# Plane copies, PSUM banks and convolution weights moved within the first pass of a two-layer attention kernel

## The chip, the cores and the metric

The kernel runs on one core of a Trainium2 chip. A core has a matrix engine (TensorE, PE in the profile), a vector engine (VectorE, DVE), a scalar engine (ScalarE, ACT), a general engine (GpSimd, POOL) and a queue that mostly issues transfers (SyncE, SP). Each works through its own instructions in their order and waits for the others by semaphores. The metric is the device time of one execution in microseconds (us), as the median of several runs.

## The reference

x has 8 images of 256 channels and 64 x 64 pixels. Two layers are applied, each added to its input.

```python
# layer 0: attention over a coarse grid
xr = conv(x, w_sr, stride 4)             # 16 x 16 positions
xr = (xr - mean) / sqrt(var + eps) * norm_g + norm_b
q = w_q @ x ; k, v = split(w_kv @ xr)    # 8 heads of 32
out = softmax(q k^T * 32**-0.5) v
x = x + gamma_s * (w_out @ out)
# layer 1: linear attention
qkv = w_qkv @ x                          # 768 channels
agg = w_pw (grouped 8 x 8) of depthwise 5 x 5 of qkv
q, k, v = groups of 8 of [qkv, agg] ; q, k = relu
kv = k^T [v, 1] ; att = q kv / (its last column + eps)
x = x + batchnorm(w_proj @ att)
```

All of it is in float32.

## The kernel before

Three passes follow each other. The first computes layer 0 and layer 1's qkv and writes q, k and v to DRAM as "planes" (q and k on a padded grid), `kd` and `vd`; the second does the depthwise and grouped convolutions and the sums k^T v; the third divides and projects. Only the first is touched.

The first pass (`first_pass`) walks over 128 steps n = (image b, strip s of 512 pixels, half c of the channels, which is four heads): 16 iterations per image. In the loop at the end of the function one iteration writes down, in this order: the first scores (`scores(..., 0, ...)`, L832: 16 matrix products into four PSUM banks, then four exponentials, L844); the work kept in `late`; for step n-1 the products with v (`valued`, L863) and the counting of the softmax sums (`counted`, L888); the second scores (`scores(..., 1, ...)`) with four more exponentials; copies of the products with v (`copied`, L895, on ScalarE) and their division (`normed`: transposes L904 on VectorE, reciprocal, product L910); then up to seven products of layer 1's qkv (L972), two or four taps of the convolution of the next image (`keys_values`, L738), the next q (L815), and for every second step the output projection (`added`, L925, L926).

Layer 1's qkv of a pair of strips (g) is three groups of seven products (pair 1, pair 2, pair 0), written down over four iterations as 7, 4, 7 and 3. A group combines products on VectorE (`part`, L1041, L1045, L1054), beginning with a copy of the first product by ScalarE (L1034). Pair 1 (k) writes a tile `whole` (L988), which one iteration later is transposed (`turn`, L992) and copied by ScalarE into the padded plane (`inside`, L998: the plane copies, four per group). Planes, k and v are then stored (`stored`, L1005, L1015, L1020). `new_stages` (L951, L952) clears the borders on GpSimd.

PSUM has eight banks. `bank` takes the first of a list and puts it at the end at once; a bank that is kept (the two of the products with v, the one of the convolution) comes back to the end of the list only with `given_back`. So the place of that call decides which earlier tile a later product must wait for.

The convolution of the next image runs over iterations 6 to 9 of an image, two taps at two places in each, with one weight tile of 256 KB per tap in three buffers (`wsr`, L735). Images 1 to 7 are done so; that of image 0 stands alone at the start.

The order on each queue is not only that of the program. A scheduler may move an instruction within its engine's stream where no data forbid it; `tc.keep_in_program_order` pins an instruction behind the one that was written down just before it on the same engine, and does not pin that other one.

```python
    def given_back(keep):
        turns.append(kept.pop(keep))
```

Of the kernel before, what the change touches and what calls it, by code (L numbers as in the profile page):

```python
# [32 lines left out]
P = 128  # L33
# [3 lines left out]
R = 4  # L37
# [582 lines left out]
def phase(dy, dx):  # L620

    return dy // 2 * 8 + dx // 2 * 4 + dy % 2 * 2 + dx % 2
# [4 lines left out]
def first_pass(ctx: ExitStack, tc: tile.TileContext, a, fine, planes, x2d, kd, vd, ready):  # L627
# [94 lines left out]
            tc.keep_in_program_order(nc.sync.dma_start(v[1 : NB2 + 1, i], src[:NB2]))  # L722


    kks, vvs = {}, {}

    def keys_values(b):
        ln = lambda name: keys.tile([P, 2, NK], F32, tag="ln", name=f"{name}_{b}", bufs=2)
        xr = ln("xr")

        ps = bank(f"sr_{b}", "sr").rearrange("p (o k) -> p o k", o=2)
        taps = sorted((phase(dy, dx), dy * R + dx) for dy in range(R) for dx in range(R))
        for f, tap in taps:
            w = keys.tile([P, 2, C], F32, tag="wsr", name=f"wsr_{b}_{f}", bufs=3)
            nc.sync.dma_start(w, a.w_sr[:, :, tap])  # L735
            for ci in range(2):
                for oc in range(2):
                    nc.tensor.matmul(  # L738
                        ps[:, oc],
                        w[:, ci, oc * P : (oc + 1) * P],  # L740
                        strips(b, f // 2)[:, ci, f % 2 * NK : (f % 2 + 1) * NK],
                        start=(f == ci == oc == 0),
                        stop=(f == R * R - 1 and ci == 1),
                        skip_group_check=True,
                    )
            yield
        nc.scalar.copy(xr, ps)
        given_back("sr")
        yield

        mean = bank(f"mean_{b}")[:, :NK]
        for ci in range(2):
            nc.tensor.matmul(mean, mean_w, xr[:, ci], start=(ci == 0), stop=(ci == 1))
        for ci in range(2):
            nc.vector.tensor_sub(xr[:, ci], xr[:, ci], mean)
        sq = ln("sq")
        nc.vector.tensor_mul(sq, xr, xr)
        yield

        var = bank(f"var_{b}")  # L760
        for kc in range(2):
            for ci in range(2):
                nc.tensor.matmul(
                    var[:, kc : kc + 1],
                    sq[:, ci, kc * P : (kc + 1) * P],
                    mean_w[:, 0:1],
                    start=(ci == 0),
                    stop=(ci == 1),
                )
        rstd = two.tile([P, 2, 2], F32, tag="rstd", name=f"rstd_{b}")  # L770
        nc.vector.tensor_scalar_add(rstd[:, 0], var[:, 0:2], LN_EPS)
        nc.gpsimd.tensor_tensor(rstd[:, 1], rstd[:, 0], mhalf, ALU.pow)
        wide = keys.tile([P, 2, P], F32, tag="wide", name=f"wide_{b}", bufs=1)
        nc.scalar.copy(wide, rstd[:, 1].unsqueeze(2).to_broadcast([P, 2, P]))
        yield
        yield
        rs = bank(f"rs_{b}")[:, :NK]
        for kc in range(2):
            nc.tensor.matmul(rs[:, kc * P : (kc + 1) * P], wide[:, kc], ident, start=True, stop=True)
        for ci in range(2):  # L780
            nc.vector.tensor_mul(xr[:, ci], xr[:, ci], rs)
            nc.vector.tensor_scalar(
                xr[:, ci], xr[:, ci], consts["vec"][:, 0, ci : ci + 1], consts["vec"][:, 1, ci : ci + 1], ALU.mult, ALU.add
            )
        yield
        kk = two.tile([P, 2, NK], F32, tag="kk", name=f"kk_{b}")
        vv = two.tile([P, 4, C], F32, tag="vv", name=f"vv_{b}")
        kks[b], vvs[b] = kk, vv
        for oc in range(2):
            ps = bank(f"k_{b}_{oc}")[:, :NK]  # L790
            for ci in range(2):
                nc.tensor.matmul(
                    ps, consts["wkv"][:, ci, oc * P : (oc + 1) * P], xr[:, ci], start=(ci == 0), stop=(ci == 1)
                )
            nc.scalar.copy(kk[:, oc], ps)
        yield
        for kc in range(2):
            ps = bank(f"v_{b}_{kc}")[:, :C]
            for ci in range(2):
                nc.tensor.matmul(  # L800
                    ps, xr[:, ci, kc * P : (kc + 1) * P], consts["wkv"][:, ci, C:], start=(ci == 0), stop=(ci == 1)
                )
            for h, rows in enumerate(HALVES):
                nc.scalar.copy(vv[rows, 2 * kc + h], ps[rows])
        for h, rows in enumerate(HALVES):
            nc.sync.dma_start(vv[HALVES[1 - h], h::2], vv[rows, h::2])
        yield
# [18 lines left out]
    def scores(b, s, c, kc, qs):  # L826
        scs = [bank(f"sc_{b}_{s}_{c}_{kc}_{h}") for h in range(4)]
        for kq in range(2 * kc, 2 * kc + 2):
            for h in range(4):
                rows = slice(h * D0, (h + 1) * D0)  # L830
                for half in range(2):
                    nc.tensor.matmul(  # L832
                        scs[h][HALVES[half], QH[kq % 2]],
                        kks[b][rows, c, kq * P // 2 : (kq + 1) * P // 2],
                        qs[rows, QH[half]],
                        start=True,
                        stop=True,
                    )
        es = []
        for h in range(4):  # L840
            if h % 2 == 0:
                e = two.tile([P, 2, 2, QB // 2], F32, tag="e", name=f"e_{b}_{s}_{c}_{kc}_{h}", bufs=E_BUFS)
                es.append(e)
            nc.scalar.activation(e[:, h % 2].rearrange("p q n -> p (q n)"), scs[h], AF.Exp, scale=D0**-0.5)  # L844
        return es

    sums, att = {}, {}

    late = []

    def catch_up():
        was, late[:] = list(late), []
        for f in was:
            f()
# [30 lines left out]
    def counted(b, s, c, es):  # L885
        for h in range(4):
            for half, rows in enumerate(HALVES):
                nc.tensor.matmul(  # L888
                    sums["av"][half][h * D0 : (h + 1) * D0, QH[1]], ones_w[rows], es[h // 2][rows, h % 2], start=True, stop=True
                )  # L890

    def copied(b, s, c):
# [64 lines left out]
    def qkv(b, g, pair):  # L957
# [21 lines left out]
        def ended(r, h, u, ps, op=ALU.add):  # L979
            if stages:  # L980
                y, x = g // 2, g % 2
                inside = stages[r][:, 2 * h : 2 * h + 2, y : y + NB, x : x + NB]
            rows = lambda t: t.rearrange("p (f y x) -> p f y x", f=2, y=NB)
            if not turned:
                nc.vector.tensor_tensor(inside, rows(u), rows(ps), op)  # L985
                return
            whole = halves.tile([P, QB], F32, tag="whole", name=f"whole_{name}_{r}_{h}", bufs=6)
            nc.vector.tensor_tensor(whole, u, ps, op)  # L988

            def turn():  # L990
                tc.keep_in_program_order(
                    nc.vector.transpose(  # L992
                        turned[r][:, :, 2 * h : 2 * h + 2].rearrange("p y f e -> p f y e"),
                        whole.rearrange("p (f y e) -> p f y e", f=2, y=NB // 2),
                    )
                )
                if stages:
                    tc.keep_in_program_order(nc.scalar.copy(inside, rows(whole)))  # L998

            late.append(turn)  # L1000

        def stored(r):
            j = js[r]
            if stages:
                nc.sync.dma_start(  # L1005
                    planes[b, j].rearrange("g (k i f) e -> g k i (f e)", k=4, i=D1)[:, g],
                    stages[r].rearrange("p f y x -> p (f y x)"),
                )
            if not turned:
                return  # L1010
            for k in range(4):
                n, src = 4 * (j % 2) + k, turned[r][k * D0 : (k + 1) * D0].rearrange("p y f e -> p y (f e)")
                if j < 4:
# [7 lines left out]

        def ready(r):
            if turned:
                late.append(lambda: stored(r))
            else:
                stored(r)

# [70 lines left out]
    for n in range(n_all + 6):  # L1098
# [2 lines left out]
        filled = now and n // 16 + 1 < B  # L1101
        if filled and at == 5 and n > 16:
            load_x(n // 16 + 1)
        if filled and at == 6:
            ahead = keys_values(n // 16 + 1)
        if now and at == (10 if n < 16 else 1):
            border(n // 16)

# [2 lines left out]
            ej[n] = joined(*order[n], e0)  # L1111
        if (n, 0) in blank:
            new_stages(*blank.pop((n, 0)), 0)
        catch_up()
        if was:
            p = order[n - 1]
            for kc in range(2):
                valued(*p, kc, es[n - 1][kc])
            counted(*p, ej.pop(n - 1))
            es.pop(n - 1)  # L1120
        if now:
            es[n] = e0, scores(*order[n], 1, q.pop(n))
            joined_too(ej[n], es[n][1])
        if (n, 1) in blank:
            new_stages(*blank.pop((n, 1)), 1)
        if was:
            copied(*p)
            normed(*p)

        products = todo.pop(n, [])  # L1130
        taps = 2 if filled and 6 <= at < 10 else 0
# [922 lines left out]
```

## Time and profile before

| | |
|---|---|
| median of three runs | 3593.32 us (3591.59 to 3598.89) |
| profiled execution, its own time | 3592.86 us |
| its span, first to last instruction | 3591.0 us |
| TensorE busy | 3490.9 us, 97% |
| VectorE, GpSimd, ScalarE busy | 2261.4, 1865.7, 1478.1 us |
| mean granted TensorE clock | 0.989 |

The first pass ends near 1960 us of the span. A row of the timeline has the start, the length, the engine, the line, the operation, the tiles it writes and reads, their shapes and how many equal instructions were merged; in brackets, the idle time before it and what ended that. A row of the waits has the engine and line that waited, what it waited for, the total, how often, and the longest. "PEq", "SPq" and so on are an engine's sequencer, "PEld" the loading of weights into TensorE. In float32 each matrix product appears as two instructions.

### The profile page before, as it was taken

The numbers are of one execution on the slowest core, as the hardware profiler recorded it, in microseconds if no ns is written. First come the engines' busy times: TensorE is split into PE (matmuls) and PEld (weight loads), VectorE is DVE, ScalarE is ACT, GpSimd is POOL, SyncE is SP. The second block draws the span as 40 slices with busy tenths as digits, with TensorE's granted clock in tenths as the row PEclk, the third lists the DMA queues.
The fourth block names the chain that finished last, engine by engine and source line by source line (L and its number), as shares of the span: only waits on it lengthen the run. The fifth ranks groups of instructions, "written<-read, shape, count | busy, mean of one in ns | idle before, by whom it ended". The sixth has DMA issues, their size and how long they took to land.

```text
span 3591.0 us, 91344 instructions
## 1 busy us (share of the span) xinstructions
PE 3490.9 (97%) x38050; PEld 2109.8 (59%) x38050; DVE 2261.4 (63%) x3499; ACT 1478.1 (41%) x3385; POOL 1865.7 (52%) x1762
## 2 busy tenths in 40 slices
PE   8999999999999999999998999999999999999998
PEld 5554555545545555455444788888888873333333
DVE  1567476575674765765777777777777774544442
ACT  2345354353443443544553444444444423333322
POOL 3557466465564664655764566656656541222222
PEclk9999999999999999999999999999999999999999
DMA  5345445455454453553655999989999987787773
GB/s 181 99 117 150 132 106 161 107 157 135 106 155 124 109 163 105 156 133 94 162 123 142 269 265 263 266 253 253 264 263 260 260 245 210 223 236 225 231 216 93
DMA packets 577192, 647.27 MB, mean 180 GB/s; under 512 B 81665, under 2 KB 452865, under 8 KB 576769
## 3 DMA queue, kind: packets, MB, share of 16 engines
q1 hardware_dynamic: 576768, 641.34, 64.5%
q8 instruction: 301, 4.93, 0.6%
q14 instruction: 123, 1.00, 0.1%
HBM read 389.85 MB, written 249.23 MB: 178 GB/s over the span
## 4 chain that ended last, share of the span: by engine, by line
PE 86%; DMA 6%; DVE 2%; ACT 2%; issue 1%; SPq 1%; POOL 1%; POOLq 0%; DVEq 0%; ACTq 0%
PE qkv L972 15%; PE p L1772 11%; PE cv L1345 8%; PE sc L832 7%; PE cv L1376 6%; PE av L863 6%; PE sums L1431 6%; PE sr L738 6%; PE o L925 6%; PE q L815 6%; PE rep L1758 2%; PE av L888 2%; DMA vq<-v 1%; DMA wsr<-in_w_sr_dram 1%; PE den L1739 1%
## 5 line engine op out<-in xcount | busy, mean ns | idle before, releaser
L883 POOL TENSOR_TENSOR ef<-ef,e 128x512 f32<-128x512 f32 x512 | 687.5, 1353 | 149.4 <-ACT e L844 126.2
L844 ACT ACTIVATE e<-sc 128x512 f32<-128x512 f32 x1024 | 529.7, 608 | 509.4 <-PE sc L832 509.3
L876 POOL TENSOR_TENSOR ef<-e 128x512 f32<-128x512 f32 x256 | 333.1, 1320 | 516.2 <-ACT e L844 476.2
L1782 POOL TENSOR_TENSOR y<-z,xs 128x512 f32<-128x512 f32 x128 | 165.4, 1301 | 459.3 <-ACT z L1780 438.7
L1345 PE MATMUL cv<-w,c 128*128 128x128 f32 x3072 | 387.1, 279 | 8.6 <-DVE stage L985 6.1
L1345 PEld LDWEIGHTS cv<-w,c 128*128 128x128 f32 x3072 | 364.5, 194 | 10.4 <-issue 6.1
L904 DVE STREAM_TRANSPOSE rden<-av 128x256 f32<-128x256 f32 x256 | 99.6, 428 | 339.8 <-ACT att L895 339.8
L972 PE MATMUL qkv<-differences,combined 128*128 128x512 f32 x576 | 291.2, 597 | 11.0 <-ACT e L844 10.4
L832 PE MATMUL sc<-q,kk 32*64 32x256 f32 x8192 | 288.3, 388 | 0.0
L1431 PE MATMUL sums<-vq,r 128*32 128x288 f32 x4096 | 265.6, 408 | 0.1
L738 PE MATMUL sr<-x,wsr 128*128 128x256 f32 x1024 | 239.0, 388 | 20.0 <-DMA wsr<-in_w_sr_dram 19.9
L1772 PE MATMUL p<-raw,wp 128*128 128x512 f32 x512 | 248.8, 608 | 6.5 <-ACT z L1780 6.4
L863 PE MATMUL av<-e,vv 64*32 64x256 f32 x8192 | 252.0, 379 | 0.7 <-ACT e L844 0.5
L1362 ACT ACTIVATE r<-s 128x512 f32<-128x512 f32 x128 | 80.9, 632 | 416.6 <-DVE s L1361 415.0
L832 PEld LDWEIGHTS sc<-q,kk 32*64 32x64 f32 x8192 | 152.1, 131 | 153.3 <-issue 105.0
L815 PE MATMUL q<-x,wq 128*128 128x512 f32 x512 | 242.0, 594 | 0.0
L738 PEld LDWEIGHTS sr<-x,wsr 128*128 128x128 f32 x1024 | 197.8, 194 | 75.0 <-issue 24.9
L1772 PE MATMUL p<-agg,wp 128*128 128x512 f32 x512 | 241.0, 593 | 0.0
L925 PE MATMUL o<-att,wout 128*128 128x512 f32 x512 | 230.4, 592 | 0.0
L823 ACT COPY q<-q 128x512 f32<-128x512 f32 x128 | 75.1, 587 | 352.2 <-PE q L815 352.2
L1376 PE MATMUL cv<-y,w 128*128 128x128 f32 x1536 | 204.4, 279 | 3.6 <-DVE y L1297 3.2
L910 DVE TENSOR_TENSOR att<-att,rall 128x512 f32<-128x512 f32 x128 | 204.9, 1600 | 4.4
(163 smaller groups left out, 6070.6 us busy)
## 6 DMA issues: line engine op xcount, KB each, us to landing
planes<-stage SPq DMA_DIRECT2D x128, 578.0 KB
d<-planes SPq DMA_DIRECT2D x128, 578.0 KB
vq<-v SPq DMA_DIRECT2D x256, 256.0 KB
raw<-planes SPq DMA_DIRECT2D x64, 578.0 KB
x<-in_xp_dram SPq DMA_DIRECT2D x64, 512.0 KB
wsr<-in_w_sr_dram SPq DMA_DIRECT2D x128, 256.0 KB
x<-x SPq DMA_DIRECT2D x128, 256.0 KB
k<-turned SPq DMA_DIRECT2D x256, 128.0 KB
```

The costliest lines, as they stand in the source:

```text
L738: nc.tensor.matmul(ps[:, oc], w[:, ci, oc * P : (oc + 1) * P], strips(b, f // 2)[:, ci, f % 2 * NK : (f % 2 + 1) * NK], start=(f == ci == ...
L815: nc.tensor.matmul(ps, consts["wq"][:, ci, c * P : (c + 1) * P], strips(b, s)[:, ci], start=(ci == 0), stop=(ci == 1),)
L832: nc.tensor.matmul(scs[h][HALVES[half], QH[kq % 2]], kks[b][rows, c, kq * P // 2 : (kq + 1) * P // 2], qs[rows, QH[half]], start=True, sto ...
L844: nc.scalar.activation(e[:, h % 2].rearrange("p q n -> p (q n)"), scs[h], AF.Exp, scale=D0**-0.5)
L863: nc.tensor.matmul(sums["av"][half][cols, : QB // 2], vvs[b][rows, kq, c * P + h * D0 : c * P + (h + 1) * D0], es[h // 2][rows, h % 2, kq ...
L883: tc.keep_in_program_order(nc.gpsimd.tensor_tensor(f, f, e[:, :, half], ALU.add))
L925: nc.tensor.matmul(ps, consts["wout"][:, c, oc * P : (oc + 1) * P], att[c], start=(c == 0), stop=(c == 1))
L972: nc.tensor.matmul(ps, w, x, start=True, stop=True)
L1345: nc.tensor.matmul(ps[:, g * P : (g + 1) * P], c[:, g, cols], w[:, g, n * P : (n + 1) * P], start=(da == 0), stop=(da == 1),)
L1376: nc.tensor.matmul(out, w[:, g], x, start=True, stop=True)
L1431: nc.tensor.matmul(ps[h * D0 : (h + 1) * D0, : 36 * D1].rearrange("p (r n e) -> p r n e", r=3, e=D1), kt[:, par, h, 2 * r + c], vq[:, r : ...
L1772: nc.tensor.matmul(as_block(ps, i // 2), wp[:, i, oc * P : (oc + 1) * P], block(g, i // 2, i % 2, j), start=(i == 0), stop=(i == 3),)
```

## The change

Four things are edited in the first pass.

- The plane copies of pair 1 and the stores of those planes go into a second list, `later`, which is worked off after the second scores and their exponentials; `late` stays where it was.
- `copied` and `normed` of step n-1 are written down ahead of the second scores, so the two banks of the products with v are given back before the second scores take theirs.
- The convolution's weights: three taps are loaded at iteration 5 (with a first `next(ahead)` there), and each tap's products are followed by the load of the tap three further on. The loads are pinned in SP's queue.
- The products of scores, of counting and of the convolution are pinned in program order. The products with v are not.

```diff
+        for f in range(3):
+            load_tap(f)
+        if b:
+            yield
         ps = bank(f"sr_{b}", "sr").rearrange("p (o k) -> p o k", o=2)
-        taps = sorted((phase(dy, dx), dy * R + dx) for dy in range(R) for dx in range(R))
-        for f, tap in taps:
-            w = keys.tile([P, 2, C], F32, tag="wsr", name=f"wsr_{b}_{f}", bufs=3)
-            nc.sync.dma_start(w, a.w_sr[:, :, tap])
+        for f in range(R * R):
+            w = ws.pop(f)
             for ci in range(2):
                 for oc in range(2):
-                    nc.tensor.matmul(
...
+                    pinned(
+                        nc.tensor.matmul(
...
+            load_tap(f + 3)
             yield
```

```diff
+        def load_tap(f):
+            if f < R * R:
+                ws[f] = keys.tile([P, 2, C], F32, tag="wsr", name=f"wsr_{b}_{f}", bufs=3)
+                tc.keep_in_program_order(nc.sync.dma_start(ws[f], a.w_sr[:, :, taps[f][1]]))
```

`scores` and `counted` put `pinned(...)` around their `nc.tensor.matmul` in the same way. In `qkv` and in the loop:

```diff
-                if stages:
-                    tc.keep_in_program_order(nc.scalar.copy(inside, rows(whole)))
+
+            def inner():
+                tc.keep_in_program_order(nc.scalar.copy(inside, rows(whole)))
 
             late.append(turn)
+            if stages:
+                later.append(inner)
...
             if turned:
-                late.append(lambda: stored(r))
+                late.append(lambda: turned_stored(r))
+                if stages:
+                    later.append(lambda: stored(r))
             else:
                 stored(r)
...
-        if filled and at == 6:
+        if filled and at == 5:
             ahead = keys_values(n // 16 + 1)
+            next(ahead)
...
-        catch_up()
+        catch_up(late)
         if was:
             p = order[n - 1]
             for kc in range(2):
                 valued(*p, kc, es[n - 1][kc])
             counted(*p, ej.pop(n - 1))
             es.pop(n - 1)
+            copied(*p)
+            normed(*p)
         if now:
             es[n] = e0, scores(*order[n], 1, q.pop(n))
             joined_too(ej[n], es[n][1])
+        catch_up(later)
         if (n, 1) in blank:
             new_stages(*blank.pop((n, 1)), 1)
-        if was:
-            copied(*p)
-            normed(*p)
```

`stored` now only stores planes; `turned_stored` holds the stores of k and v.

More of the change, by code (lines that the diff above doesn't have):

```diff
@@ L722, in border @@
             tc.keep_in_program_order(nc.sync.dma_start(v[1 : NB2 + 1, i], src[:NB2]))
+    pinned = tc.keep_in_program_order
     kks, vvs = {}, {}
@@ L729, in keys_values @@
         xr = ln("xr")
+        taps = sorted((phase(dy, dx), dy * R + dx) for dy in range(R) for dx in range(R))
+        ws = {}
+        def load_tap(f):
[6 more added lines that the diff above has]
+            yield
         ps = bank(f"sr_{b}", "sr").rearrange("p (o k) -> p o k", o=2)
-        taps = sorted((phase(dy, dx), dy * R + dx) for dy in range(R) for dx in range(R))
-        for f, tap in taps:
-            w = keys.tile([P, 2, C], F32, tag="wsr", name=f"wsr_{b}_{f}", bufs=3)
-            nc.sync.dma_start(w, a.w_sr[:, :, tap])
+        for f in range(R * R):
+            w = ws.pop(f)
             for ci in range(2):
                 for oc in range(2):
[L738 to L744, printed above, removed]
+                    pinned(
+                        nc.tensor.matmul(
+                            ps[:, oc],
+                            w[:, ci, oc * P : (oc + 1) * P],
+                            strips(b, f // 2)[:, ci, f % 2 * NK : (f % 2 + 1) * NK],
+                            start=(f == ci == oc == 0),
+                            stop=(f == R * R - 1 and ci == 1),
+                            skip_group_check=True,
+                        )
                     )
+            load_tap(f + 3)
             yield
@@ L831, in scores @@
                 for half in range(2):
[L832 to L837, printed above, removed]
+                    pinned(
+                        nc.tensor.matmul(
+                            scs[h][HALVES[half], QH[kq % 2]],
+                            kks[b][rows, c, kq * P // 2 : (kq + 1) * P // 2],
+                            qs[rows, QH[half]],
+                            start=True,
+                            stop=True,
+                        )
                     )
@@ L847, in first_pass, with catch_up @@
     sums, att = {}, {}
-    late = []
-    def catch_up():
+    late, later = [], []
+    def catch_up(late):
         was, late[:] = list(late), []
@@ L887, in counted @@
             for half, rows in enumerate(HALVES):
-                nc.tensor.matmul(
-                    sums["av"][half][h * D0 : (h + 1) * D0, QH[1]], ones_w[rows], es[h // 2][rows, h % 2], start=True, stop=True
+                pinned(
+                    nc.tensor.matmul(
+                        sums["av"][half][h * D0 : (h + 1) * D0, QH[1]],
+                        ones_w[rows],
+                        es[h // 2][rows, h % 2],
+                        start=True,
+                        stop=True,
+                    )
                 )
@@ L996, in turn, with turned_stored @@
                 )
-                if stages:
-                    tc.keep_in_program_order(nc.scalar.copy(inside, rows(whole)))
+            def inner():
+                tc.keep_in_program_order(nc.scalar.copy(inside, rows(whole)))
             late.append(turn)
+            if stages:
+                later.append(inner)
         def stored(r):
-            j = js[r]
[L1004 to L1010, printed above, removed]
+            nc.sync.dma_start(
+                planes[b, js[r]].rearrange("g (k i f) e -> g k i (f e)", k=4, i=D1)[:, g],
+                stages[r].rearrange("p f y x -> p (f y x)"),
+            )
+        def turned_stored(r):
+            j = js[r]
             for k in range(4):
```

## The prediction

> **What bounds the kernel now.** I read the page first, then the waits of TensorE in the first pass, then the timeline around those waits. The page says that TensorE (PE) is the busy engine:
>
> ```profile
> PE 3490.9 (97%) x38050; PEld 2109.8 (59%) x38050; DVE 2261.4 (63%) x3499; ACT 1478.1 (41%) x3385; POOL 1865.7 (52%) x1762
> ```
>
> No other engine is near, so only time in which PE stands can be won. The table of stretches puts 1832.04 of 1865.00 us busy between 70 and 1935 us, the first pass without its start and end. What PE waits for there:
>
> ```profile
> PE qkv L972 <- ACT e L844: 19.4, 31, 1.3
> PE sr L738 <- DMA wsr<-in_w_sr_dram: 11.8, 7, 2.2
> ```
>
> 31 waits of products for an exponential, and 7 for convolution weights: the two places that the change touches. Busy ends are modelled, so I take losses from distances between starts. An undisturbed iteration beside one with plane copies (PE timeline):
>
> ```profile
> 964.61 1.98 PE L972 MATMUL qkv<-x,wqkv 128*128 128x512 f32 x4
> 966.43 1.02 PE L972 MATMUL qkv<-differences,combined 128*128 128x512 f32 x2
> 967.29 1.89 PE L800 MATMUL v<-wkv,xr 128*128 128x256 f32 x8
> ...
> 978.67 1.98 PE L972 MATMUL qkv<-x,wqkv 128*128 128x512 f32 x4
> 981.09 1.13 PE L972 MATMUL qkv<-differences,combined 128*128 128x512 f32 x2 [0.43 <-ACT e L844]
> 982.05 1.88 PE L815 MATMUL q<-x,wq 128*128 128x512 f32 x4
> ```
>
> Three products take 967.29 - 964.61 = 2.68 us undisturbed, and 982.05 - 978.67 = 3.38 in the other: 0.70 lost where the profile shows 0.43 idle. ScalarE (ACT) tells why:
>
> ```profile
> 977.81 2.19 ACT L998 COPY stage<-whole 128x512 f32<-128x512 f32 x4
> 979.87 0.67 ACT L895 COPY att<-av 128x256 f32<-128x256 f32 x2
> 980.40 2.10 ACT L844 ACTIVATE e<-sc 128x512 f32<-128x512 f32 x4
> ```
>
> Four plane copies (2.19) stand ahead of the second exponentials, and the third product needs the bank that the first of those empties. The same once per batch where a bank is lent to the convolution, so that already the second product needs it:
>
> ```profile
> 440.81 1.13 PE L972 MATMUL qkv<-x,wqkv 128*128 128x512 f32 x2
> 443.22 1.12 PE L972 MATMUL qkv<-x,wqkv 128*128 128x512 f32 x2 [1.29 <-ACT e L844]
> ```
>
> There the next q row starts at 445.04: 4.23 against 2.68, 1.55 lost. The weights' wait, in iteration 9 of a batch, PE and then SP's queue:
>
> ```profile
> 411.57 1.12 PE L832 MATMUL sc<-q,kk 32*64 32x256 f32 x32
> 414.37 0.60 PE L888 MATMUL av<-ef,ones_w 64*32 64x256 f32 x4
> 416.13 3.87 PE L738 MATMUL sr<-x,wsr 128*128 128x256 f32 x16 [1.16 <-DMA wsr<-in_w_sr_dram]
> 420.51 1.12 PE L832 MATMUL sc<-q,kk 32*64 32x256 f32 x32
> 421.56 1.98 PE L972 MATMUL qkv<-x,wqkv 128*128 128x512 f32 x4
> ```
> ```profile
> 410.74 2.06 SPq L929 DMA_DIRECT2D x<-x  x2
> 412.89 22.41 SPq L735 DMA_DIRECT2D wsr<-in_w_sr_dram  x8
> ```
>
> The load of tap 10 is issued at 412.89, behind two stores of x that wait for VectorE, and PE starts on it 3.24 us later.
>
> [...] here rden starts at 980.30 right behind the first att copy. [...] Here a step from packed products to full ones takes about 0.3 us where the pitch is 0.22, so each extra switch costs some 0.09.
>
> **The change, part by part.**
>
> Plane copies behind the second exponentials. ACT's order becomes first exponentials, att copies, second exponentials, plane copies, then the part copy. The second exponentials then start when the scores are done, 978.67 + 0.13, and not at 980.40. ACT's work is the same; it idles some 0.6 us more before those exponentials, so the part copy ends near 983.6 instead of 982.97. VectorE, whose next product waits for it, was busy to 983.49: 0.1 us late at most, and PE returns to that bank only after 988. The planes' two stores move behind all eight stores of k. The weights of taps 3 and 4 follow them: about 608.5 to 609 in the batch where before shows 608.57, with tap 3 needed near 613.9. Cost nothing while that margin holds; bounds 0 to 1 us a batch if it doesn't.
>
> Banks of av given back ahead of the second scores. The rotation now gives the second or third product a bank of av. Worked out for the row above: counting ends 977.62, att copies 977.9 to 978.6, transposes to 979.4; the third product is due at 980.39, a margin of 1.0 us. In iteration 10 (440.81) the second product is due at 441.67, its bank free near 441.0. Products from the fourth on get banks of the second exponentials, which then end over 1.5 us earlier than before. So both waits go: 24 x 0.70 + 7 x 1.55 = 27.7 us. In either way alone most of this would go too; together they count once.
>
> Taps three ahead, and pins. Tap 10's load now stands behind the first store of v, about 395, and taps 11 and 12 ahead of the x stores, about 406.5: both landed before 411. But pinning scores, counting and convolution without pinning the products with v lets the scheduler reorder iteration 9. In the built program its PE order is tap 10, products with v, counting, one head of the second scores, tap 11, first scores, the other heads of the second scores. First scores and second scores become neighbours, and three heads of the second write the banks that the first exponentials must empty. What hid those (products with v and counting, 2.3 us) is gone. Price: each first exponential starts 1.21 us after its scores (974.26 to 975.47), lasts 0.61, pitch (2.06 - 0.61)/3 = 0.48; the third ends 1.21 + 0.61 + 0.97 = 2.79 after the first scores start. Where scores follow scores at the start of the trace,
>
> ```profile
> 56.21 4.32 PE L832 MATMUL sc<-q,kk 32*64 32x256 f32 x96
> 60.46 0.66 PE L863 MATMUL av<-e,vv 64*32 64x256 f32 x16
> ```
>
> the next product begins 1.07 after the fourth exponential, the last awaited there (exponentials from 57.33, so 59.39). So first scores to first product takes 2.79 + 1.07 = 3.86 us, not 2 x 1.05 = 2.10. The rest of iteration 9: tap 10 1.82, products with v 1.75, counting 0.57, the single head 0.52 (two passes and a switch, estimate), tap 11 1.82, less 0.09 for the switch at the front: 6.39. Sum 10.25. Before, from first scores to first product in the seven batches: 12.35, 9.99, 9.81, 10.75, 10.18, 10.76, 12.60, sum 76.44. After 7 x 10.25 = 71.75: 4.7 us won, where with neither stall nor split (taps 3.55, products 1.75, counting 0.57, scores 2.10, less 0.09: 7.88) it would be 76.44 - 55.16 = 21.3. GpSimd's additions of these exponentials start 6 us later and end near 429; the counting that needs them comes at 439.
>
> Start and end. At the start only one strip of x changes place with tap 2, and the third tap needs both: 0. At the end the stores of the last planes stand behind eight k stores (0.5 to 1.0 us each from 1946.5, so 1951 to 1954.7, where the copies end at 1951.96 and before issued the later one at 1954.91), and the second pass begins behind their landing: 1.5 us later to 2 earlier, I take 0.
>
> Sum: 27.7 + 4.7 = 32.4 us from the profiled execution's 3592.86: 3560.5. The median of the runs stands 0.46 above it: 3561.
>
> **Rivals.**
>
> (1) The new stall is absent or small, because scores and exponentials overlap better than at the trace's start: up to 21.3 - 4.7 = 16.6 more, 3545 to 3552. Against it: the exponentials' pitch is ScalarE's own.
>
> (2) The early banks don't serve: a product waits for VectorE's transposes instead, and half the 27.7 stays: 3575. For it: rden waits for att in nearly every iteration; against it: the margin of 0.7 to 1.0 us.
>
> (3) Everything won in one place comes back in another, mainly iteration 9 with 4.6 us more a batch: within 0.2% (7 us, about what these runs can tell).
>
> (4) Slower: weights come late behind other transfers. Tap 3 now follows the planes (2 x 578 KB) directly, and taps 0 to 2 are loaded at iteration 5 behind x instead of long before. To lose 32.4 + 7.2 over seven batches, tap 3 must be 5.7 us late in each: landing at 619.6, 11 us after issue. Tap 10 took 3.24, and DMA engines are 0.37 to 0.44 busy from 612 to 620. It decides from there only; with half of it the result is still faster, near 3580.
>
> **How the numbers follow.** Forecast 3561: 0.70, its own range 3554 to 3568. Rival 1: 0.10. Rival 2, with smaller late weights: 0.13. Rival 3: 0.04. Rival 4: 0.03. Faster 0.93, same 0.04, slower 0.03. Range: 3550 to 3576, which takes in rival 2 and the unknown bounds, and leaves out the lower part of rival 1 and rivals 3 and 4.
>
> **What would show it.** Right: no wait of products for an exponential in the first pass; second exponentials right behind the second scores; no wait for weights at tap 10; in iteration 9 scores behind scores, 10 us to the first product; second and third pass as before. Wrong: products waiting for rden or att, a weights wait at taps 0, 3 or 4, or an iteration 9 over 12 us.

## The result, and the profile after

| | before | after |
|---|---|---|
| median of four runs each, same chip | 3592.45 us (3590.75 to 3598.89) | 3562.03 us (3555.48 to 3566.68) |
| profiled execution, its own time | 3592.86 us | 3560.51 us |
| first pass, first scores to last qkv product, from the starts in the PE timeline | 1896.6 us | 1864.3 us |

The ratio is 0.9911, with a 95% interval of 0.9890 to 0.9931. The forecast was 3561.

The page's line of busy times of the changed kernel:

```profile
PE 3481.9 (98%) x38050; PEld 2111.5 (59%) x38050; DVE 2278.5 (64%) x3499; ACT 1478.1 (42%) x3385; POOL 1858.6 (52%) x1762
```

As many instructions as before, and a span of 3558.6 us, 32.4 less. The page puts 23 of these to time in which TensorE stood (3591.0 - 3490.9 before, 3558.6 - 3481.9 now) and 9 to its busy time. Part of a wait counts as busy there (0.43 us shown idle before where 0.70 is lost by the starts), and so do products at half clock (below). The waits of PE from 70 to 1910 us, the first pass without its start and end:

```profile
PE sc L847 <- ACT e L860: 5.2, 7, 0.7
PE av L905 <- POOL ef L899: 1.8, 2, 1.0
PE qkv L994 <- POOL differences L964: 0.6, 1, 0.6
```

The two large rows of before are gone. The new one that matters is the first: in iteration 9 of seven batches (a batch is the sixteen iterations of one image) scores (L847) wait for exponentials. (Lines have shifted: scores are L847 for L832, exponentials L860 for L844, products with v L879, counting L905, qkv L994, convolution L750, weights' load L738, copies of av L917, plane copies L1021.)

An iteration with plane copies, the PE timeline and then ACT's:

```profile
961.72 1.12 PE L847 MATMUL sc<-q,kk 32*64 32x256 f32 x32
962.77 1.98 PE L994 MATMUL qkv<-x,wqkv 128*128 128x512 f32 x4
964.59 1.02 PE L994 MATMUL qkv<-differences,combined 128*128 128x512 f32 x2
965.45 1.88 PE L829 MATMUL q<-x,wq 128*128 128x512 f32 x4
```
```profile
961.91 0.65 ACT L917 COPY att<-av 128x256 f32<-128x256 f32 x2
962.91 2.06 ACT L860 ACTIVATE e<-sc 128x512 f32<-128x512 f32 x4 [0.35 <-PE sc L847]
964.83 2.20 ACT L1021 COPY stage<-whole 128x512 f32<-128x512 f32 x4
```

Second exponentials now start 0.14 us after the product that follows their scores (962.91 against 962.77), with the copies behind them, and three products take 965.45 - 962.77 = 2.68 us, the undisturbed value. It is 2.68 in all 31 places that lost 0.70 or 1.55 before.

Iteration 9, PE and then SP's queue:

```profile
407.94 0.65 PE L847 MATMUL sc<-q,kk 32*64 32x256 f32 x4
408.52 1.99 PE L750 MATMUL sr<-x,wsr 128*128 128x256 f32 x8
410.44 1.12 PE L847 MATMUL sc<-q,kk 32*64 32x256 f32 x32
412.30 2.06 PE L847 MATMUL sc<-q,kk 32*64 32x256 f32 x28 [0.74 <-ACT e L860]
414.29 1.98 PE L994 MATMUL qkv<-x,wqkv 128*128 128x512 f32 x4
```
```profile
399.25 3.38 SPq L738 DMA_DIRECT2D wsr<-in_w_sr_dram  x2
403.07 2.06 SPq L951 DMA_DIRECT2D x<-x  x2
```

One head of the second scores, tap 11, first scores, and the other three heads behind them, which wait for banks of the first exponentials: 414.29 - 410.44 = 3.85 us to the first product, in all seven batches. The weights are there. The loads of taps 10, 11 and 12, issued from 412.89 on before, behind the stores of x, now stand ahead of them: tap 10's is issued at 388.20, and those of taps 11 and 12 are the two in the first row.

### The profile page after: what moved, and what is told of

Same layout as the page of the kernel before. It is cut to its first block, busy times and chain, and to the rows that moved or that the text cites. A ratio compares the mean times of both kernels' runs of the same rounds, so it can differ in the third digit from the quotient of the medians.

```text
span 3558.6 us, 91293 instructions
## 1 busy us (share of the span) xinstructions
PE 3481.9 (98%) x38050; PEld 2111.5 (59%) x38050; DVE 2278.5 (64%) x3499; ACT 1478.1 (42%) x3385; POOL 1858.6 (52%) x1762
## 4 chain that ended last, share of the span: by engine, by line
PE 88%; DMA 5%; DVE 3%; ACT 1%; POOL 1%; issue 1%; SPq 1%; POOLq 0%; DVEq 0%; ACTq 0%
PE qkv L994 16%; PE p L1799 11%; PE cv L1372 8%; PE sc L847 8%; PE av L879 7%; PE cv L1403 6%; PE o L947 6%; PE q L829 6%; PE sr L750 6%; PE sums L1458 6%; PE rep L1785 2%; DMA raw<-planes 2%; PE av L905 2%; PE raw L1441 1%; PE den L1766 1%; DMA vq<-v 1%
## 5 line engine op out<-in xcount | busy, mean ns | idle before, releaser
L860 ACT ACTIVATE e<-sc 128x512 f32<-128x512 f32 x1024 | 528.4, 604 | 508.9 <-PE sc L847 508.9
L847 PE MATMUL sc<-q,kk 32*64 32x256 f32 x8192 | 298.5, 387 | 5.6 <-ACT e L860 5.2
L994 PE MATMUL qkv<-differences,combined 128*128 128x512 f32 x576 | 288.7, 592 | 0.6 <-POOL differences L964 0.6
L879 PE MATMUL av<-e,vv 64*32 64x256 f32 x8192 | 252.4, 379 | 0.0
L847 PEld LDWEIGHTS sc<-q,kk 32*64 32x64 f32 x8192 | 155.4, 131 | 162.9 <-issue 101.4
L750 PE MATMUL sr<-x,wsr 128*128 128x256 f32 x1024 | 235.6, 382 | 8.7 <-DMA wsr<-in_w_sr_dram 8.6
L750 PEld LDWEIGHTS sr<-x,wsr 128*128 128x128 f32 x1024 | 194.8, 191 | 64.4 <-issue 38.2
L932 DVE TENSOR_TENSOR att<-att,rall 128x512 f32<-128x512 f32 x128 | 217.9, 1702 | 4.4
L1010 DVE TENSOR_TENSOR whole<-part,qkv 128x512 f32<-128x512 f32 x256 | 172.3, 683 | 65.9 <-ACT part L1060 49.2
```

Of the source, the lines that this page charges most:

```text
L750: nc.tensor.matmul(ps[:, oc], w[:, ci, oc * P : (oc + 1) * P], strips(b, f // 2)[:, ci, f % 2 * NK : (f % 2 + 1) * NK], start=(f == ci == ...
L847: nc.tensor.matmul(scs[h][HALVES[half], QH[kq % 2]], kks[b][rows, c, kq * P // 2 : (kq + 1) * P // 2], qs[rows, QH[half]], start=True, sto ...
L879: nc.tensor.matmul(sums["av"][half][cols, : QB // 2], vvs[b][rows, kq, c * P + h * D0 : c * P + (h + 1) * D0], es[h // 2][rows, h % 2, kq ...
L994: nc.tensor.matmul(ps, w, x, start=True, stop=True)
```

## Experiments

My theory, the forecast's: the first pass wins 27.7 us from the second exponentials and 4.7 from iteration 9, where a new stall, made by pinning the neighbours of the products with v but not them, takes back 16.6. Rivals: either edit of the second half of an iteration would do; the stall has another cause or belongs to all pins; loads ahead are what wins in iteration 9.

All ratios are to before, on the same chip, with 95% intervals. "First pass" is measured as in the table above, in one execution each; it repeats better than the whole time, because the second and third passes differ from execution to execution (below).

| kernel | first pass, us | median, us | ratio |
|---|---|---|---|
| copies_only | 1866.7 | 3554.64 | 0.9903 [0.9874, 0.9933] |
| banks_only | 1882.6 | 3579.96 | 0.9974 [0.9962, 0.9986] |
| copies_banks | 1865.2 | 3551.95 | 0.9892 [0.9860, 0.9925] |
| pin_all | 1847.7 | 3542.72 | 0.9862 [0.9825, 0.9898] |
| no_pins | 1851.8 | 3546.70 | 0.9880 [0.9845, 0.9916] |
| pins_late_banks | 1846.9 | 3542.78 | 0.9872 [0.9842, 0.9903] |
| pin_late | 1848.5 | 3543.40 | 0.9865 [0.9834, 0.9896] |
| pins_old_loads | 1896.6 | 3583.51 | 0.9989 [0.9975, 1.0003] |
| weights_only | 1896.9 | 3588.71 | 1.0001 [0.9989, 1.0014] |
| weights_again | 1893.8 | 3591.84 | 1.0006 [0.9991, 1.0022] |
| weights_pinned | 1875.1 | 3566.99 | 0.9948 [0.9928, 0.9967] |

**The copies, the banks, both.** Against before, copies_only moves the plane copies and their stores alone; banks_only moves `copied` and `normed` alone; copies_banks does both. The weights' part and the pins are left out of all three.

```diff
 copies_only:
-        catch_up()
+        catch_up(late)
...
+        catch_up(later)
 banks_only:
             es.pop(n - 1)
+            copied(*p)
+            normed(*p)
...
-        if was:
-            copied(*p)
-            normed(*p)
```

> The kernel before with the plane copies and their stores moved behind the second exponentials, nothing else. My theory: the first of the second exponentials then ends near 979.4, before the third product is due at 980.4, and in iteration 10 near 441.6, before the second product at 441.8; so nearly all of the 27.7 us goes by this edit alone: 3564 to 3568 us; the weights' wait in iteration 9 (11.8 us shown) stays. Rival: the early banks do the work and the copies alone give at most 10 us: 3582 to 3590.

> The kernel before with the two banks of the products with v given back ahead of the second scores, nothing else; the order of every engine stays as before, only the banks differ. My theory: the third product then waits for the first transpose of av, which stands behind plane and att copies and ends at 980.73 (0.4 lost instead of 0.70), and in iteration 10 near 442.9 (1.25 lost instead of 1.55): about 9 us less than before, 3582 to 3586 us, and the wait of products names VectorE's transposes. Rival: the early banks alone free the products: 3564 to 3568 us, no such wait.

> Both edits of the second half of an iteration, without the weights and pins. My theory: the copies alone take away all 27.7 us, so that the banks add nothing: first pass 1866 to 1867 us as with the copies alone, the seven waits for weights (12 us) still there, time 3555 to 3564. If the banks do add something, it shows as a first pass shorter than 1865.

With the copies alone, all 31 places are back at 2.68 us, and PE's row of waits for weights stays (12.0 us, 7). The first pass is as expected. The time lies some 10 us under what was expected, and in the profiled execution that is not in the first pass: from its last product to the end of the span it took 1628.0 us, before's 1638.2. Some 2 us of that is an earlier start of the second pass (below). The rest of that part has the same code in both, and it varies: weights_only and weights_again are one program, and took 1643.8 and 1629.1. So a single time is not to be read to a few us here.

The banks alone leave two thirds of the lost time, under another name. The waits of PE have a row for the seven places where the second product is held up:

```profile
PE qkv L972 <- DVE rden L904: 7.0, 7, 1.0
```

The same iteration, in the timelines of ACT, DVE, PEld and PE of banks_only:

```profile
972.92 2.19 ACT L998 COPY stage<-whole 128x512 f32<-128x512 f32 x4
974.99 0.66 ACT L895 COPY att<-av 128x256 f32<-128x256 f32 x2
...
975.42 0.78 DVE L904 STREAM_TRANSPOSE rden<-av 128x256 f32<-128x256 f32 x2 [2.31 <-ACT att L895]
...
975.92 0.30 PEld L972 LDWEIGHTS qkv<-differences,combined 128*128 128x128 f32 x2 [0.97 <-DVE rden L904]
975.92 1.12 PE L972 MATMUL qkv<-differences,combined 128*128 128x512 f32 x2
```

The product no longer waits for an exponential, but for a bank of av. (In the other 24 places, of which this is one, PE's own gap is 0.14 us, too short for a row, but its load of weights waits 0.97 us for rden, VectorE's transpose.) That bank is copied by ScalarE and then transposed by VectorE, one behind the other, and ScalarE's copies of it stand behind the same plane copies. (rden starts 0.43 us after the first of the two copies starts, which takes 0.39.) Of 0.70 us, 0.41 stays, and of 1.55, 1.27: 24 x 0.29 + 7 x 0.28 = 8.9 of 27.7 us are won.

Both together take 1865.2 us, 1.5 less than the copies alone. Iteration 9 explains it: from first scores to first product its seven batches sum to 73.6 us here and 75.1 there (76.4 before, 72.3 in banks_only). The weights come a little earlier or later in each execution, and one thing more differs. Before, in two of the seven batches:

```profile
174.66 5.41 PE L738 MATMUL sr<-x,wsr 128*128 128x256 f32 x16 [1.99 <-DMA wsr<-in_w_sr_dram]
180.00 0.65 PE L888 MATMUL av<-ef,ones_w 64*32 64x256 f32 x12
```

Behind the wait, taps 10 and 11 take 180.00 - 174.66 = 5.34 us where 3.65 is usual, and TensorE's granted clock stands at 0.50, half speed, for 3.4 us. The other is at 1619 us; together they lost 3.4 us. copies_only and copies_banks have one such stretch each, banks_only none. The banks add nothing once the copies are moved.

**The pins.** pin_all pins the products with v as well; no_pins drops all of the change's pins on TensorE and keeps those on the loads.

```diff
 pin_all, in valued:
-                    nc.tensor.matmul(
-                        sums["av"][half][cols, : QB // 2],
...
+                    pinned(
+                        nc.tensor.matmul(
+                            sums["av"][half][cols, : QB // 2],
...
 no_pins:
-    pinned = tc.keep_in_program_order
+    pinned = lambda ins: ins
```

> The changed kernel with the products with v pinned too, so that in iteration 9 the order is taps 10 and 11, first scores, products with v, counting, second scores. My theory: the stall of scores behind scores (0.74 us shown idle, 3.85 instead of 2.10 us from first scores to first product) goes, iteration 9 takes 7.9 instead of 10.4 us in seven batches: 17 to 18 us less than the changed kernel, 3542 to 3546 us. Rival: the stall only covers a wait for weights of taps 10 and 11, which then shows in its place: within 5 us of the changed kernel, 3557 to 3565.

> The changed kernel with none of its products pinned (loads still three taps ahead). The built order of iteration 9 is tap 10, first scores, half of the products with v, tap 11, the rest, counting, second scores. My theory: the pins, not the loads ahead, made the stall; iteration 9 takes about 8.4 us (7.9 and three more switches between packed and full products), some 14 us less than the changed kernel, 3546 to 3550 us. Rival: the stall comes from the loads ahead and stays: 3558 to 3565 us.

Iteration 9 of pin_all, PE timeline:

```profile
407.37 1.12 PE L847 MATMUL sc<-q,kk 32*64 32x256 f32 x32
408.42 1.96 PE L880 MATMUL av<-e,vv 64*32 64x256 f32 x64
410.17 0.64 PE L907 MATMUL av<-ef,ones_w 64*32 64x256 f32 x16
410.74 1.12 PE L847 MATMUL sc<-q,kk 32*64 32x256 f32 x32
411.79 1.98 PE L996 MATMUL qkv<-x,wqkv 128*128 128x512 f32 x4
```

Products with v and counting are back between the two scores, and scores wait for no exponential there. The first pass is 1864.3 - 1847.7 = 16.6 us shorter than with the change, the sum that the forecast had set on the stall and the split (21.3 - 4.7). By the starts: a batch of the change takes 10.39 us to its first product (below), without stall and split 7.88, so 7 x 2.51 = 17.6, less 1.1 for weights that come late in two batches of pin_all. With no pin on TensorE the pass is 12.5 us shorter than the change's: the scheduler then puts tap 10 ahead of the first scores, tap 11 amid the products with v, and scores do not meet scores. So the stall belongs to the half set of pins, not to pins or early loads as such. Their medians, 3542.7 and 3546.7 us, lie below the kernel before and the changed one; which of the two is the better their intervals don't tell.

**What of pin_all is needed.** pins_late_banks is pin_all with `copied` and `normed` back behind the second exponentials. pin_late pins on TensorE only from iteration 4 on, to save two waits of scores for q at the start of pin_all (1.5 us together, ending at 72 and 91 us). pins_old_loads is pin_all with each tap's load written down at the tap and not pinned, from iteration 6, as before.

```diff
 pin_late:
-    pinned = tc.keep_in_program_order
+    pins = [False]
+    pinned = lambda ins: tc.keep_in_program_order(ins) if pins[0] else ins
...
+        pins[0] = n >= 4
 pins_old_loads:
+            w = keys.tile([P, 2, C], F32, tag="wsr", name=f"wsr_{b}_{f}", bufs=3)
+            nc.sync.dma_start(w, a.w_sr[:, :, taps[f][1]])
...
-            load_tap(f + 3)
```

> The kernel with all products pinned (pin_all), but the two banks given back behind the second scores as before; the order of every engine is that of pin_all. My theory: with the plane copies out of the way the banks give nothing, the second exponentials free theirs in time (margin 1.0 us for the third product, some 0.1 us for the second in iteration 10): first pass within 2 us of pin_all, and no wait of products for an exponential over 0.2 us. Rival: the banks are needed, 0.4 us lost in each of 31 iterations, 12 us.

> pin_all with the pins in force from iteration 4 on, so that at the very start products with v may again stand ahead of first scores that wait for q. My theory: the two waits there (scores for q, 1.5 us in pin_all) go, 1 to 3 us less than pin_all in the first pass, in all 3538 to 3543 us. Rival: start and end of those waits only move and nothing changes: within 1 us.

> pin_all with each tap's load written just ahead of its products and left to the scheduler, as before; the order of TensorE is that of pin_all. My theory: tap 10's load is again issued behind the two stores of x, lands 4.5 to 5.6 us after tap 10 is due, and with nothing left between them TensorE waits all of it: 35 to 40 us more than pin_all, 3576 to 3584 us. Rival: the loads' place hardly matters once the order of TensorE is fixed: within 10 us of pin_all.

Without the early banks the first pass is 1846.9 us, as with them: they have no effect there either. Pinning late makes the first pass no shorter; the rival's "within 1 us" holds. My reading of that start was wrong. From the first scores to the sixth q row, eleven of the thirteen kernels take 20.3 to 20.4 us, pin_all as well as copies_only and banks_only, which pin nothing on TensorE. Only before and pin_late take 21.2, and those two have TensorE's granted clock at 0.50 from 66 to 69 us. So the pins cost nothing there, and leaving them out gains nothing. With the old loads everything that the pins won is lost. The waits of PE, and iteration 9 in its timeline:

```profile
PE sr L740 <- DMA wsr<-in_w_sr_dram: 31.4, 7, 4.9
```
```profile
405.32 3.60 PE L938 MATMUL o<-att,wout 128*128 128x512 f32 x8
413.26 5.20 PE L740 MATMUL sr<-x,wsr 128*128 128x256 f32 x16 [4.34 <-DMA wsr<-in_w_sr_dram]
418.39 1.12 PE L836 MATMUL sc<-q,kk 32*64 32x256 f32 x32
```

Tap 10 is pinned at the front of the iteration and its weights come 4.5 us late in the mean (31.4 over 7); by the distances between starts, tap 10 begins 32.6 us late in seven batches. Then taps 10 and 11 run in part at a granted clock of 0.50 in every batch, in stretches of 3.4 or 6.8 us that begin in the last 2 us of the wait: 418.39 - 413.26 = 5.13 us here where 3.55 is undisturbed, 17.4 us in all (they spend 33.9 us at half speed, which costs half of that). So a third of this loss is not the wait but the half clock that came with it. Together it is 50 us, and the first pass is 48.9 us longer than pin_all's (50 less its 1.1). So early loads are worth much where the order is fixed, while the order before, which the scheduler chose, had hidden most of the delay by moving those taps behind scores and products with v.

**The weights' part alone.** weights_only is the change without the copies' and the banks' move; weights_again is the same kernel once more; weights_pinned pins the products with v in it too (the edit of pin_all).

```diff
 weights_only, against the changed kernel:
-        catch_up(late)
+        catch_up()
...
-            copied(*p)
-            normed(*p)
...
-        catch_up(later)
...
+        if was:
+            copied(*p)
+            normed(*p)
```

> The kernel before with the third part alone: loads three taps ahead, and scores, counting and convolution pinned; plane copies and banks as before. My theory: the weights' wait goes and the stall of scores behind scores comes, iteration 9 takes 10.4 us in place of 10.9 on the mean, and the 27.7 us of the products stay: 2 to 6 us less than before. Rival: the part wins the whole loss of iteration 9, some 20 us.

> The kernel of weights_only once more, to see another execution. Its first execution lost what iteration 9 won: in three batches (417, 1380 and 1622 us) the six products behind the second scores took 4.38 us and not 2.68, with no wait, at matmul distances of 0.85 us and not 0.43, under a granted clock of 0.5. If that belongs to this order of the work, it is there again in some of the seven batches, 1.7 us each, the first pass (first scores to last product) is near 1897, and the time within 0.2% of before. If it was chance, no batch shows it, the first pass is near 1892 us, and the time is some 4.7 us under before.

> The weights' part alone, with the products with v pinned too; the plane copies and the banks as before. My theory: iteration 9 then has neither the wait for weights nor scores behind scores, and the waits of products for second exponentials all stay (24 of 0.7 us, 7 of 1.55). The first pass is 1847.7 (with every part and v pinned) + 27.7 + 2.0 (the end of the pass as before) = 1877 us, 19 us shorter than before, and the time 3570 to 3576. If the order of iteration 9 needs the early banks, so that second exponentials hold up its products here, it is 3577 or more. No stretch of half clock in iteration 9 if those come from the scores behind scores; some if they come from second exponentials that run close ahead of the products.

weights_only was a miss: no gain. The waits for weights are gone, and iteration 9 runs as in the change, with 3.84 us from first scores to first product. But in three of seven batches the three products behind it (six instructions) took 4.38 us and not 2.68, with no wait. The PE timeline at one of them, and the row of the table of stretches for one microsecond of it (the granted clock is the third number from the right):

```profile
417.10 3.42 PE L994 MATMUL qkv<-x,wqkv 128*128 128x512 f32 x4
420.31 1.33 PE L994 MATMUL qkv<-differences,combined 128*128 128x512 f32 x2
421.48 2.75 PE L750 MATMUL sr<-x,wsr 128*128 128x256 f32 x12
```
```profile
418.00:419.00 1.00, 1.00 (x2) 0.42 (x2) 0.96 (x2) 1.00 (x3) 1.00 (x2) 0.50 0.00 0
```

The granted clock was 0.50: a loss of 1.7 us each, 5.1 in all, which eats the 3.7 us that iteration 9 won against before (3.4 of them before's own two stretches of half clock). In weights_again one batch of seven showed it, and the first pass was 2.85 us shorter than before's: 3.7 and 0.85 (the start, below) less 1.7. That lies between the two cases that I had set. Both times agree with no gain, but their intervals (-4 to +5 us, and -3 to +8) can hardly tell 3 us. weights_pinned, without scores behind scores, had none, and its first pass is 1896.6 - 1875.1 = 21.5 us shorter, where 21.3 had been worked out for "neither stall nor split" (the start gave 0.9, late weights in one batch took 0.9). Its median is 3 us below what was expected; by the ratio it wins 18.7 us. All 31 waits for exponentials are still there (19.2 us).

## Why the prediction was right, and where it was not

**Second exponentials, 27.7 us: right in size and place.** All 31 distances went to 2.68 us. But the part said of the two edits that "in either way alone most of this would go too". That step failed for the banks: alone they won 8.9 us, because the copies of av, which free those banks, stand behind the same plane copies. The margin of 1.0 us worked out there holds only where the copies are moved, and then the banks are not needed (copies_only, pins_late_banks). The forecast counted both once, so the sum did not suffer; rival 2, a product waiting for VectorE's transposes, is what banks_only shows, and it is absent from the change.

**Iteration 9: right in kind, 1.0 us too large in sum.** 3.86 us was worked out from first scores to first product, and 3.85 measured. The terms that were mis-sized are the single head (0.52, measured 0.58) and tap 11 (1.82, measured 1.92, the switch behind it included): with tap 10 1.82, products with v 1.75, counting 0.57 and the switch, a batch takes 10.39 us and not 10.25. Won: 76.44 - 7 x 10.39 = 3.7 us and not 4.7. And most of that was luck: the 76.44 holds two batches at half clock, 12.35 and 12.60, which the part counted as won along with the waits. They account for 3.4 of the 3.7. In banks_only, with the old loads and no such stretch, the seven batches sum to 72.3, less than the change's 72.7. Rival 1, the stall absent, is what pin_all would be; its 16.6 us came out, with terms of slightly other size.

**Start and end: 0 was taken, 2.8 us measured.** From the first scores to the sixth q row the profile after needs 0.8 us less. That is not the change's doing: in before's profile TensorE's granted clock stands at 0.50 from 66 to 69 us, in that of after at 1.00, and copies_only and banks_only, which leave this start as it was, need 0.8 less too. At the end, the first convolution of the second pass begins sooner behind the last product of the first, where the profile after has

```profile
1922.54 0.38 PE L1193 MATMUL total<-both,mean_w 128*128 128x2 f32 x2 [1.90 <-DVE whole L1010]
1926.96 6.15 PE L1372 MATMUL cv<-w,c 128*128 128x128 f32 x32 [4.05 <-DVE stage L1007]
```

with an idle time of 4.05 us, for which before had 6.07. The estimate for that end reached from 1.5 later to 2 earlier; the earlier end came. It goes with the move of the plane copies and their stores: from the last product of the pass to this convolution it is 6.9 us in all eight kernels that have the move, copies_only among them, and 8.8 to 9.0 in the five that don't. With it, the later store of the last planes is issued at 1919.37, 0.7 us before the last product (1920.04); before, it stood between stores of k and was issued at 1954.91, 2.1 us after that product (1952.80).

**The sum.** 27.7 + 3.7 + 0.8 + 2.0 = 34.2 us up to the second pass, where 32.4 was forecast; the profiled execution won 32.35, since the other passes took some 1.9 us more in this one. They have differed by up to 16 us between kernels that share that code, and 4.2 of the 34.2 us are stretches of half clock in before's one profiled execution (0.8 at the start, 3.4 in iteration 9). So that the median meets the forecast within 1 us is partly luck. What the runs tell closely is the first pass.

**Late weights, rival 4:** from 70 us on no wait of PE for weights is in the first pass after. Fewer of the gains are the weights' than the forecast said: iteration 9 varied between 72.3 and 76.4 us in the four executions of kernels that have the wait, and the change takes 72.7. Against copies_banks, the weights' part with its half set of pins gave 0.8 us of first pass; with v pinned too it gives 17.5 (1865.2 - 1847.7). In device time nothing shows a gain of the half-pinned part either: the medians of copies_only and copies_banks, 3554.64 and 3551.95 us, lie below the changed kernel's 3562.03, and the intervals of their ratios overlap with its own. What the change won, as far as the runs tell, is the move of the plane copies.

## What to carry to other kernels

Before pinning some instructions of an engine in program order, look at what stands between them: one left unpinned may be moved away, and if it was the cover of a wait, the wait comes out (0.74 us shown idle in each of seven batches here); pin all of the group or none (here either was 12 us or more better in the first pass than the half set). Where two edits aim at one wait, follow each bank back to the engine that frees it, through that engine's own queue, since one of the two may wait behind the same work as the thing it replaces (banks_only won 8.9 of 27.7 us). A time to be explained may hold stretches of half clock that the next execution has not (three in iteration 9 of weights_only, one in weights_again): look at the clock beside each place before its loss is given to a wait. Loads put ahead pay when the order of their users is fixed (48.9 us from pins_old_loads to pin_all), and much less when a scheduler had already moved those users back (13.4 from copies_banks to no_pins).

## What was not expected of the hardware

TensorE's granted clock fell to half for about 3.4 us (1.7 us lost at half speed) in 3 and 1 of 7 batches in two executions of one program, right behind the scores of iteration 9, in which PE had stood idle for 0.74 us. Elsewhere such stretches came behind waits for weights: in all seven batches of pins_old_loads (waits of 4.3 to 4.9 us), and before behind waits of 1.99 and 2.24 us, but not behind those of 2.07 and 2.08. Such stretches decide differences of 1 to 5 us between two executions (0.8 at the start of before, 5.1 in weights_only); the table of stretches shows them, a list of waits does not. What sets them off is not shown. The length of a wait alone does not tell: 1.99 us had one behind it, 2.08 had none. In weights_only the 3.84 us ahead held 60 instructions of packed score products (32 x 64 tiles) and 0.74 us of idle time. The change has the same iteration 9 and none of it in its one profile; why is open.
